# Layer 3 of a four-layer graph network: both of its weight products as seven block products, with the weight combinations streamed from DRAM

## Chip, core and metric

The kernel runs on one core of a Trainium2 chip. The metric is the device time of one execution in microseconds (us). Everything is 32-bit floating point.

TensorE (PE in the profile) multiplies, VectorE (DVE), ScalarE (ACT) and GpSimd (POOL) do the elementwise work, and SyncE (SP) issues DMA transfers. Products land in PSUM, eight banks of 128 partitions x 512 floats; everything else lives in SBUF.

## What is computed

The input x has 128 graphs of 64 nodes with 512 features. Four graph layers run one after the other, each followed by a residual and a layer norm:

```
x = layernorm(x + L0(x, adj, w, a))            # attention from one score per node
x = layernorm(x + L1(x, adj, Wq, Wk, Wv, ...)) # attention from x Wq Wk^T x^T, times adj
x = layernorm(x + L2(x, adj, mask, Wqk, Wv))   # softmax over nodes, scales x Wv
x = layernorm(x + L3(x, adj, W1, b1, gamma, beta, W2, b2))
```

Layer 3 is what the change is about. With H = (adj != 0) and the degree factors D and B:

```
def hypergraph_conv(x, adj, W, b):
    xw = x @ W.T
    m = Be * (H.T @ xw)
    return Dn * (H @ m) + b
h = relu(hypergraph_conv(x, adj, W1, b1))      # 512 -> 1024
h = layer_norm(h, gamma, beta)
y = hypergraph_conv(h, adj, W2, b2)            # 1024 -> 512
return y + x
```

## The kernel before

**Tiles and groups.** Two graphs make a tile of 128 nodes, two tiles (GT = 2) make a group of 256 nodes, and there are 32 groups (NG). `run(g)` at L361 is a generator that takes one group through all four layers. It stops at 15 yields, so it has 16 stages. Up to four groups are in flight (IN_FLIGHT), four stages apart (APART), and the main loop at L515 advances each of them by one stage in every step, the youngest first. So in one step in four the stages that stand side by side are, for example, the gather of layer 0, the scores of layers 1 and 2, and the first product of layer 3 (L485). Two steps later comes the second product of layer 3 (L506), beside the transposes of layers 1 and 2 (L278) and layer 2's product with its value weights (L464). One round of four steps finishes one group.

**Order of the instructions.** The program states only the operations and their buffers. A scheduler puts each engine's instructions in an order ahead of time, mostly by the order of the program but also by when it expects operands and buffers to be ready, and adds the waits. On the chip that order is fixed.

**Buffers.** A pool of n buffers under one name hands out a new buffer when an older one has been released by its last reader. In PSUM before the change: four buffers `mm` (the products), two `tr` (transposes and gathers), two `sm` (small results: scores, row sums, softmax), which are all eight banks.

**Layer 3 before.** `gathered(xt, gm)` at L470 multiplies the group's features by the normalised two-step adjacency `gm` and leaves the transposed result `gT`. The stage at L485 multiplies it by w3a, which lies in SBUF as a whole (512 x 1024): for each of two tiles and two halves of 512 columns, four matmuls over 128 rows of the weight. VectorE adds the bias, ScalarE applies the relu, VectorE takes the statistics. After the normalisation (L493) the gather at L502 makes `ghT`, and L506 multiplies by w3b (1024 x 512, in SBUF, with gamma folded in at L217): for each of two tiles eight matmuls of 512 columns. The result is added to `xt`, which already holds the residual (L472 to L477, on GpSimd). Then come the last layer norm and the store.

**Block-diagonal matrices.** The adjacency of a tile is two 64 x 64 blocks. Before the change three things are written as 128 x 128 block-diagonal tiles from standing sets of zeroed buffers: the attention weights of layers 0 and 1 (`e_bd`, three buffers, `on_diagonal` at L354), H for the product that makes `gm` (`h_bd`, two, L425), and `gm` itself (`g_bd`, three). `row_sums` at L324 sums over them with a matmul against ones.

**Every four groups** `prepare_chunk` at L232 prepares the adjacency of eight tiles. It needs four `mm` buffers through `over_graph` (L222).

Where a statement stands in a helper, the profile gives the helper's line: L296 is `product` (all products by w0, w_v1, w_v2, w3a, w3b), L305 `product_T` (the projections), L320 `scores`, L327 `row_sums`, L278 `transposed`, L288 `gathered`, L346 the end of `layer_norm`. L374 is layer 0's score product, L419 layer 1's product with the values, L440 the product of layer 2's softmax, L443 and L447 its maximum and exponential, L458 the product for `gm`.

Of the kernel before, what the change touches and what calls it, by code (L numbers as in the profile page):

```python
# [24 lines left out]
IN_FLIGHT = 4  # L25
EPS = 1e-5
# [5 lines left out]
def kernel(  # L32
# [31 lines left out]
    ps_mm = ctx.enter_context(tc.tile_pool(name="ps_mm", bufs=4, space=bass.MemoryType.PSUM))  # L64
    ps_tr = ctx.enter_context(tc.tile_pool(name="ps_tr", bufs=2, space=bass.MemoryType.PSUM))
    ps_sm = ctx.enter_context(tc.tile_pool(name="ps_sm", bufs=2, space=bass.MemoryType.PSUM))
# [33 lines left out]
    next_e = diagonals("e_bd", 3)  # L100
    next_h = diagonals("h_bd", 2)
# [46 lines left out]
    w3a_sb = weights(w3a, D, DH, "w3a_sb")  # L148
# [3 lines left out]
    w3b_sb = weights(w3b, DH, D, "w3b_sb")  # L152
# [56 lines left out]
    def prepare_3():  # L209

        ps = ps_mm.tile([P, D], FP, name="mm")
        for c in range(KH):
            nc.tensor.matmul(ps, beta_c[:, c : c + 1].to_broadcast([P, P]), w3b_sb[:, c, :],
                             start=(c == 0), stop=(c == KH - 1))
        nc.scalar.copy(bw_b, ps)
        for c in range(KH):
            nc.vector.tensor_scalar(w3b_sb[:, c, :], w3b_sb[:, c, :], gamma_c[:, c : c + 1], None, ALU.mult)  # L217
# [106 lines left out]
    def row_sums(bd):  # L324
        ps = ps_sm.tile([P, GT, P], FP, name="sm")
        for t in range(GT):
            nc.tensor.matmul(ps[:, t, 0:1], bd[:, t, :], ones, start=True, stop=True)  # L327
        return ps[:, :, 0]

# [31 lines left out]
    def run(g):  # L361
# [23 lines left out]
        nc.vector.reciprocal(f, row_sums(bd))  # L385
# [27 lines left out]
        bd = on_diagonal(next_e(), e, adj)  # L413
        yield
        f = small.tile([P, GT], FP, name="f")
        nc.vector.reciprocal(f, row_sums(bd))
        for t in range(GT):
            po = ps_mm.tile([P, D], FP, name="mm")
            nc.tensor.matmul(po, bd[:, t, :], v[:, t, :], start=True, stop=True)  # L419
            nc.vector.scalar_tensor_tensor(xt[:, t, :], po, f[:, t : t + 1], xt[:, t, :], ALU.mult, ALU.add)  # L420
        layer_norm(xt)

        h_bd = next_h()
        for rows, cols in halves:
            nc.vector.tensor_scalar(h_bd[rows, :, cols], adj[rows], 0.0, None, ALU.not_equal)  # L425
# [31 lines left out]
        for t in range(GT):  # L457
            nc.tensor.matmul(pg[:, t, :N], h_bd[:, t, :], bhd[:, t, :], start=True, stop=True)  # L458
# [13 lines left out]
        for t in range(GT):  # L472
            c = work.tile([P, D], FP, name="junk")
            nc.gpsimd.tensor_scalar(c, bw_b, g1[:, t : t + 1], 1.0, ALU.mult, ALU.mult)
            nc.gpsimd.tensor_add(c, c, b3b_b)
            nc.gpsimd.tensor_scalar(xt[:, t, :], xt[:, t, :], 2.0, 0.0, ALU.mult, ALU.add)  # L476
            nc.gpsimd.tensor_add(xt[:, t, :], xt[:, t, :], c)  # L477
        yield
        h = stage.tile([P, GT, DH], FP, name="h")
        st = small.tile([P, GT, DH // D, 6], FP, name="st3")  # L480
        mv = small.tile([P, GT, 2], FP, name="mv")
        for t in range(GT):
            for i in range(DH // D):
                hi = h[:, t, ts(i, D)]
                nc.vector.tensor_add(hi, product(gT, t, w3a_sb, ts(i, D)), b3a_b[:, ts(i, D)])  # L485
                nc.scalar.activation(hi, hi, AF.Relu)  # L486
                nc.vector.bn_stats(st[:, t, i, :], hi)  # L487
            nc.vector.bn_aggr(mv[:, t, :], st[:, t].rearrange("p i s -> p (i s)"))
# [8 lines left out]
        for t in range(GT):  # L497
            ghT.append(work.tile([P, KH, P], FP, name="ghT"))
            for i in range(KH // KC):
# [3 lines left out]
                nc.scalar.copy(ghT[t][:, ts(i, KC), :], tr)  # L503
        yield
        for t in range(GT):
            nc.vector.tensor_add(xt[:, t, :], product(ghT[t], 0, w3b_sb, chunks=KH), xt[:, t, :])  # L506
# [8 lines left out]
    while g < NG or running:  # L515
# [14 lines left out]
        if step == 4:  # L530
            prepare_2()
        if step == 7:
            prepare_3()
# [42 lines left out]
```

## Time and profile before

| | us |
|---|---|
| median of three runs | 2632.75 (2632.62 to 2634.61) |
| profiled execution | 2635.76 |
| its span in the profile | 2634.0 |
| DVE L342, the layer norms' statistics, x256 | 176.0 |
| DVE L346, their last step, x256 | 185.3 |
| DVE L485, bias of the first product, x128 | 88.5 |
| DVE L487, its statistics, x128 | 88.8 |
| DVE L506, end of the second product, x64 | 44.3 |
| POOL L402, L474, L475, L476, L477 together | 351.8 |
| ACT L503, copies of ghT, x128 | 75.0 |
| mean clock of TensorE | 0.998 of full |

A row of a group gives line, engine, operation, what it writes and reads (names without buffer numbers), the shapes and the count; then its busy time, the mean duration in ns, and after the second bar how long the engine had stood idle just before these instructions and what ended most of that. PE is TensorE's matmuls, PEld its weight loads, which overlap them. A row of the timeline starts with the start and the length of a run of equal instructions. A row of the chain has the same two numbers and what was on the path. A row of the view of windows has the stretch, its length, and for PE, PEld, DVE, ACT and POOL in turn the busy time with the count of instructions, then TensorE's clock, the share of DMA and its GB/s.

DMA is nearly unused after the start: 19 GB/s on average, 217 in the first fortieth of the span.

### The profile page before, as it was taken

How to read it: one execution, taken by the hardware profiler on the slowest of the kernel's cores; microseconds unless marked ns; L12 is line 12 of the kernel's file. 1: busy time of each engine (PE TensorE's matmuls, PEld its weight loads, DVE VectorE, ACT ScalarE, POOL GpSimd, SP SyncE). 2: the span in 40 equal slices, each digit the busy share in tenths (PEclk: the TensorE clock that was granted, in tenths of full speed). 3: DMA queues.
4: the chain of work that ended last, by engine and by line, in shares of the span. 5: the costliest groups of instructions: out<-in, count | busy, mean ns of one | idle time of the engine just before them, and what ended most of it. 6: DMA issues, size and time to landing. Idle time of an engine off the chain costs nothing.

```text
span 2634.0 us, 27593 instructions
## 1 busy us (share of the span) xinstructions
PE 2556.3 (97%) x11272; PEld 1544.1 (59%) x11272; DVE 1138.0 (43%) x2552; ACT 590.6 (22%) x1164; POOL 546.8 (21%) x560
## 2 busy tenths in 40 slices
PE   6999999999999999999999999999999999999998
PEld 4565565655565655565655565655665655665654
DVE  3535453445433455433545434445443445433443
ACT  0222221222221222221122221222221222221221
POOL 4211221212211222211312212212212212211211
PEclk9999999999999999999999999999999999999999
DMA  5000000000000000000000000000000000000000
GB/s 217 32 1 17 5 17 17 16 17 13 8 16 17 21 17 8 10 17 20 17 16 4 14 21 17 17 17 1 17 16 17 17 17 0 17 16 8 9 9 16
DMA packets 22190, 50.31 MB, mean 19 GB/s; under 512 B 1504, under 2 KB 1504, under 8 KB 22064
## 3 DMA queue, kind: packets, MB, share of 16 engines
q1 hardware_dynamic: 18560, 35.66, 4.0%
q0 software_dynamic: 3504, 12.89, 1.3%
q8 instruction: 89, 1.46, 0.2%
q14 instruction: 37, 0.30, 0.0%
HBM read 31.76 MB, written 16.78 MB: 18 GB/s over the span
## 4 chain that ended last, share of the span: by engine, by line
PE 87%; DVE 5%; issue 5%; POOL 3%; DMA 0%; ACT 0%; POOLq 0%; DVEq 0%
PE mm L296 57%; PE mm L305 17%; PE tr L288 4%; PE sm L320 2%; POOL rstd L335 2%; DVE x L346 2%; PE tr L278 1%; DVE x L420 1%; PE mm L169 1%; PE mm L225 1%; DVE x L389 1%; PE mm L419 1%; PE sm L327 1%; PE sm L374 0%; DMA junk<-in_a_dram 0%
## 5 line engine op out<-in xcount | busy, mean ns | idle before, releaser
L296 PE MATMUL mm<-wv_sb,xT 128*128 128x512 f32 x1024 | 460.6, 593 | 0.0
L305 PE MATMUL mm<-xT,m_sb 128*128 128x256 f32 x2048 | 458.3, 381 | 2.1 <-DVE hw L254 1.5
L296 PE MATMUL mm<-w3a_sb,xT 128*128 128x512 f32 x1024 | 448.0, 595 | 0.0
L296 PE MATMUL mm<-w3b_sb,ghT 128*128 128x512 f32 x1024 | 444.7, 592 | 0.0
L305 PEld LDWEIGHTS mm<-xT,m_sb 128*128 128x128 f32 x2048 | 385.7, 190 | 70.8 <-issue 17.9
L335 POOL TENSOR_TENSOR rstd<-ve,mhalf 128x2 f32<-128x2 f32 x160 | 127.7, 798 | 1369.9 <-DVE ve L333 1291.0
L296 PEld LDWEIGHTS mm<-w3b_sb,ghT 128*128 128x128 f32 x1024 | 194.5, 190 | 244.4 <-issue 244.4
L296 PEld LDWEIGHTS mm<-w3a_sb,xT 128*128 128x128 f32 x1024 | 191.9, 190 | 231.7 <-issue 229.6
L296 PEld LDWEIGHTS mm<-wv_sb,xT 128*128 128x128 f32 x1024 | 187.2, 190 | 185.8 <-issue 183.9
L385 DVE RECIPROCAL f<-sm 128x2 f32<-128x2 f32 x32 | 5.5, 171 | 617.9 <-PE sm L327 617.9
L296 PE MATMUL mm<-w_sb,xT 128*128 128x512 f32 x512 | 225.2, 593 | 0.4 <-issue 0.4
L346 DVE TENSOR_SCALAR x<-x,mv,rstd 128x512 f32<-128x512 f32 x256 | 185.3, 765 | 75.2 <-POOL rstd L335 75.2
L342 DVE BATCH_NORM_STATS2 st<-x 128x6 f32<-128x512 f32 x256 | 176.0, 688 | 4.7
L485 DVE TENSOR_TENSOR h<-mm,b3a_b 128x512 f32<-128x512 f32 x128 | 88.5, 692 | 193.4 <-PE mm L296 193.4
L296 PEld LDWEIGHTS mm<-w_sb,xT 128*128 128x128 f32 x512 | 97.0, 190 | 122.3 <-issue 122.2
L486 ACT ACTIVATE h<-h 128x512 f32<-128x512 f32 x128 | 80.6, 630 | 387.7 <-DVE h L485 387.7
L506 DVE TENSOR_TENSOR x<-mm,x 128x512 f32<-128x512 f32 x64 | 44.3, 691 | 277.0 <-PE mm L296 277.0
L476 POOL TENSOR_SCALAR x<-x 128x512 f32<-128x512 f32 x64 | 39.7, 620 | 559.9 <-PE tr L288 559.9
L502 PE MATMUL tr<-g_bd,h 128*128 128x128 f32 x1024 | 125.7, 282 | 5.5 <-ACT h L493 5.5
L487 DVE BATCH_NORM_STATS2 st<-h 128x6 f32<-128x512 f32 x128 | 88.8, 694 | 88.4 <-ACT h L486 88.4
L309 ACT ACTIVATE z<-mm,r_c 128x256 f32<-128x256 f32 x128 | 60.6, 473 | 293.7 <-PE mm L305 293.7
L502 PEld LDWEIGHTS tr<-g_bd,h 128*128 128x128 f32 x1024 | 121.3, 195 | 7.7 <-ACT h L493 7.4
(138 smaller groups left out, 2374.4 us busy)
## 6 DMA issues: line engine op xcount, KB each, us to landing
x<-in_x_dram SPq DMA_DIRECT2D x32, 512.0 KB, 3.7
out_dram<-x SPq DMA_DIRECT2D x32, 512.0 KB, 2.8
adj<-in_adjT_dram SPq DMA_DIRECT2D x8, 256.0 KB, 2.8
wv_sb<-in_wv_dram POOLq DMA_DIRECT2D x2, 1024.0 KB, 15.3
w3a_sb<-in_w3a_dram POOLq DMA_DIRECT2D x1, 2048.0 KB, 17.4
w3b_sb<-in_w3b_dram POOLq DMA_DIRECT2D x1, 2048.0 KB, 16.4
h<-in_wqk_dram POOLq DMA_DIRECT2D x2, 1024.0 KB, 5.7
w_sb<-in_w_dram POOLq DMA_DIRECT2D x1, 1024.0 KB, 10.7
```

Source lines behind the costliest of these rows:

```text
L288: nc.tensor.matmul(tr[:, c, :], xt[:, t, ts(c, P)], bd[:, t, :], start=True, stop=True)
L296: nc.tensor.matmul(ps, lhsT[:, k, ts(t, P)], w[:, k, cols], start=(k == 0), stop=(k == chunks - 1))
L305: nc.tensor.matmul(pz[:, : GT * P], w[:, k, ts(c, P)], xT[:, k, :], start=(k == 0), stop=(k == KC - 1))
L309: nc.scalar.activation(zT[:, c, :], pz[:, : GT * P], AF.Identity, bias=bias[:, c : c + 1])
L320: nc.tensor.matmul(ps[rows, t, :N], zT[:, k, tok], xT[:, k, tok], start=(k == 0), stop=(k == KC - 1))
L335: nc.gpsimd.tensor_tensor(rstd, ve, mhalf, ALU.pow)
L342: nc.vector.bn_stats(st[:, t, :], xt[:, t, :])
L346: nc.vector.tensor_scalar(xt[:, t, :], xt[:, t, :], mv[:, t, 0:1], rstd[:, t : t + 1], ALU.subtract, ALU.mult)
L485: nc.vector.tensor_add(hi, product(gT, t, w3a_sb, ts(i, D)), b3a_b[:, ts(i, D)])
L486: nc.scalar.activation(hi, hi, AF.Relu)
L487: nc.vector.bn_stats(st[:, t, i, :], hi)
L502: nc.tensor.matmul(tr[:, c, :], h[:, t, ts(i * KC + c, P)], gm[:, t, :], start=True, stop=True)
```

## The change

Each product of layer 3 is divided into 2 x 2 blocks: the two tiles of the group by two halves of the input features on the left, two halves of the input features by two halves of the output columns on the right. Four output blocks would need eight block products. The change uses Winograd's form of Strassen's scheme, with seven products of sums of blocks: four sums on the left (`side_sums`) and four on the right (`combined`).

- The sums of the weights are made once (`prepare_3a`, `prepare_3b`), written to DRAM, and from then on all weight blocks are streamed: `fetch` issues on SP's queue the next of 14 pieces a group, 512 KB each, into a ring of six. The piece that follows six later is requested when a product has been issued. The two whole weights leave SBUF.
- `side_sums` makes the sums of the left side, three on VectorE and one on GpSimd, into parts of the tile `h` that are free at that time. It stands at the end of the stage before the product.
- `seven_products` keeps two PSUM accumulators (`chx`, `chz`, one bank each) over several products and reads the partial sums in between, and takes one `mm` buffer for a third. VectorE adds seven results to the four output blocks.
- PSUM: `mm` has three buffers, `chx` and `chz` one each, `tr` two, `sm` one.
- To make room, `h_bd` and one of the `e_bd` buffers go. Layer 1's attention and H stay compact tiles of 64 columns, and row sums, layer 1's product with the values and the product for `gm` are done for the two halves of 64 partitions separately.

```diff
+RING = 6
+PIECE = 1024
-    ps_mm = ctx.enter_context(tc.tile_pool(name="ps_mm", bufs=4, space=bass.MemoryType.PSUM))
+    ring = ctx.enter_context(tc.tile_pool(name="ring", bufs=RING))
+    dram = ctx.enter_context(tc.tile_pool(name="dram", bufs=1, space=bass.MemoryType.DRAM))
+    ps_mm = ctx.enter_context(tc.tile_pool(name="ps_mm", bufs=3, space=bass.MemoryType.PSUM))
+    ps_ch = ctx.enter_context(tc.tile_pool(name="ps_ch", bufs=1, space=bass.MemoryType.PSUM))
-    ps_sm = ctx.enter_context(tc.tile_pool(name="ps_sm", bufs=2, space=bass.MemoryType.PSUM))
+    ps_sm = ctx.enter_context(tc.tile_pool(name="ps_sm", bufs=1, space=bass.MemoryType.PSUM))
-    next_e = diagonals("e_bd", 3)
-    next_h = diagonals("h_bd", 2)
+    next_e = diagonals("e_bd", 2)
-    w3a_sb = weights(w3a, D, DH, "w3a_sb")
-    w3b_sb = weights(w3b, DH, D, "w3b_sb")
...
+    USE = ("b11", "b21", "t2", "t1", "t3", "b22", "t4")
+    def combined(q):
+        t1, t2 = piece_tile(), piece_tile()
+        nc.gpsimd.tensor_sub(t1, q["b12"], q["b11"])
+        nc.vector.tensor_sub(t2, q["b22"], t1)
+        t3 = piece_tile()
+        nc.gpsimd.tensor_sub(t3, q["b22"], q["b12"])
+        t4 = piece_tile()
+        nc.vector.tensor_sub(t4, q["b21"], t2)
+        return {"t1": t1, "t2": t2, "t3": t3, "t4": t4}
...
+    def fetch():
+        n = fetched[0]
+        fetched[0] += 1
+        if n >= NG * 2 * len(USE):
+            return
+        which = "ab"[n // len(USE) % 2]
+        src = pieces[which][USE[n % len(USE)]]
+        t_ = piece_tile()
...
+        nc.sync.dma_start(out=dst, in_=src)
+        on_chip.append(t_)
...
-    def row_sums(bd):
+    def row_sums(e):
         ps = ps_sm.tile([P, GT, P], FP, name="sm")
         for t in range(GT):
-            nc.tensor.matmul(ps[:, t, 0:1], bd[:, t, :], ones, start=True, stop=True)
+            for h, (rows, _) in enumerate(halves):
+                nc.tensor.matmul(ps[rows, t, 0:1], e(t, h), ones[rows], start=True, stop=True)
         return ps[:, :, 0]
+
+    def side_sums(s, a):
+        nc.vector.tensor_add(s[0], a["21"], a["22"])
+        nc.gpsimd.tensor_sub(s[2], a["11"], a["21"])
+        nc.vector.tensor_sub(s[1], s[0], a["11"])
+        nc.vector.tensor_sub(s[3], a["12"], s[1])
+
+    def seven_products(a, s, base, dst):
+        n = a["11"].shape[1]
+        def times(ps, left, first, last):
+            b = on_chip.popleft().rearrange("p (c o) -> p c o", c=n)
+            for k in range(n):
+                nc.tensor.matmul(ps, left[:, k, :], b[:, k, :], start=first and k == 0, stop=k == n - 1,
+                                 skip_group_check=True)
+            fetch()
+        w = PIECE // n
+        x = ps_ch.tile([P, D], FP, name="chx")[:, :w]
+        y = ps_mm.tile([P, D], FP, name="mm")[:, :w]
+        z = ps_ch.tile([P, D], FP, name="chz")[:, :w]
+        add = nc.vector.tensor_add
+        times(x, a["11"], True, False)
+        add(dst["11"], x, base["11"])
+        times(y, a["12"], True, True)
+        add(dst["11"], y, dst["11"])
+        times(x, s[1], False, False)
+        add(dst["12"], x, base["12"])
+        times(z, s[0], True, False)
+        add(dst["22"], z, base["22"])
+        times(x, s[2], False, False)
+        add(dst["22"], x, dst["22"])
+        times(z, s[3], False, True)
+        add(dst["12"], z, dst["12"])
+        times(x, a["22"], False, True)
+        add(dst["21"], x, base["21"])
...
-        bd = on_diagonal(next_e(), e, adj)
+        nc.vector.tensor_mul(e, e, adj)
         yield
         f = small.tile([P, GT], FP, name="f")
-        nc.vector.reciprocal(f, row_sums(bd))
+        nc.vector.reciprocal(f, row_sums(lambda t, h: e[halves[h][0], t, :]))
         for t in range(GT):
             po = ps_mm.tile([P, D], FP, name="mm")
-            nc.tensor.matmul(po, bd[:, t, :], v[:, t, :], start=True, stop=True)
+            for rows, _ in halves:
+                nc.tensor.matmul(po[rows], e[rows, t, :], v[rows, t, :], start=True, stop=True)
...
-            nc.tensor.matmul(pg[:, t, :N], h_bd[:, t, :], bhd[:, t, :], start=True, stop=True)
+            for rows, _ in halves:
+                nc.tensor.matmul(pg[rows, t, :N], hT[rows, t, :], bhd[rows, t, :], start=True, stop=True)
...
-        yield
+
         h = stage.tile([P, GT, DH], FP, name="h")
+        a = {f"{t + 1}{i + 1}": gT[:, ts(i, KC // 2), ts(t, P)] for t in range(GT) for i in range(2)}
+        room = [h[:, 1, ts(i, D // 2)].rearrange("p (k q) -> p k q", q=P) for i in (2, 3, 0, 1)]
+        side_sums(room, a)
+        yield
+        blocks = {f"{t + 1}{i + 1}": h[:, t, ts(i, D)] for t in range(GT) for i in range(2)}
+        seven_products(a, room, {k: b3a_b[:, ts(int(k[1]) - 1, D)] for k in blocks}, blocks)
...
-                nc.vector.tensor_add(hi, product(gT, t, w3a_sb, ts(i, D)), b3a_b[:, ts(i, D)])
...
-        yield
-        for t in range(GT):
-            nc.vector.tensor_add(xt[:, t, :], product(ghT[t], 0, w3b_sb, chunks=KH), xt[:, t, :])
+        a = {f"{t + 1}{i + 1}": ghT[t][:, ts(i, KC), :] for t in range(GT) for i in range(2)}
+        room = [h[:, t, ts(i, D)].rearrange("p (k q) -> p k q", q=P) for t in range(GT) for i in range(2)]
+        side_sums(room, a)
+        yield
+        blocks = {f"{t + 1}{i + 1}": xt[:, t, ts(i, D // 2)] for t in range(GT) for i in range(2)}
+        seven_products(a, room, blocks, blocks)
         layer_norm(xt)
```

## The prediction

> **What bounds the kernel now.** I read the page's first part, then its groups, then the chain of waits over one steady round, then the timeline of the tightest stretch. The page and the groups of TensorE:
>
> ```profile
> PE 2556.3 (97%) x11272; PEld 1544.1 (59%) x11272; DVE 1138.0 (43%) x2552; ACT 590.6 (22%) x1164; POOL 546.8 (21%) x560
> ...
> L296 PE MATMUL mm<-w3a_sb,xT 128*128 128x512 f32 x1024 | 448.0, 595 | 0.0
> L296 PE MATMUL mm<-w3b_sb,ghT 128*128 128x512 f32 x1024 | 444.7, 592 | 0.0
> ...
> L278 PE MATMUL tr<-ident,x 128*128 128x128 f32 x512 | 77.9, 276 | 41.6 <-DVE x L346 41.6
> ```
>
> TensorE is busy 97% of the span and the two products of layer 3 are 893 us of it. Its only steady stop is before the second transposes, L278: 41.6 us, or 1.3 us for each of the 32 groups. One f32 matmul is two instructions, hence 1024 for 512 calls. So time is gained only by taking matmul time away, and lost by any new stop of TensorE. Pieces of the chain between 1299 and 1394 us (start, length, what), which hold one round of 79.05 us (first w3a matmul at 1313.13 and 1392.18 us):
>
> ```profile
> 1300.94 6.91 PE mm L305 x32
> ...
> 1311.19 2.02 PE sm L320 x64
> ...
> 1334.00 0.34 PE sm L327 x4
> 1334.34 1.82 PE mm L419 x4
> 1336.16 0.22 PE sm L440 x2
> 1336.38 0.41 PE sm L458 x4
> ...
> 1365.02 0.38 PE sm L374 x8
> 1365.40 7.10 PE mm L305 x32
> 1372.51 6.87 PE mm L296 x16
> 1379.37 6.91 PE mm L305 x32
> ```
>
> From them come the prices: an instruction with 512 columns 6.87/16 = 0.429 us, with 256 columns 6.91/32 = 0.216 us (half, so narrower products lose nothing), a score instruction on 64 columns of the array 2.02/64 = 0.032 us. Last, the timeline after the attention of layer 1 and a count of the busy time around it:
>
> ```profile
> 1336.00 0.38 PE L440 MATMUL sm<-e,same 128*128 128x128 f32 x2
> 1336.22 0.56 PE L458 MATMUL sm<-bhd,h_bd 128*128 128x64 f32 x4
> ...
> 1340.21 0.27 DVE L443 TENSOR_REDUCE mx<-sm 128x2 f32<-128x128 f32 x1
> ...
> 1341.45 0.54 ACT L447 ACTIVATE e<-sm,mx 128x64 f32<-128x64 f32 x2
> ...
> 1342.48 2.88 DVE L346 TENSOR_SCALAR x<-x,mv,rstd 128x512 f32<-128x512 f32 x2 [0.58 <-POOL rstd L335]
> ...
> 1344.10 0.63 PE L278 MATMUL tr<-ident,x 128*128 128x128 f32 x4 [1.91 <-DVE x L346]
> ```
>
> ```profile
> 1334.00:1349.50 15.50, 13.59 (x76) 9.26 (x75) 13.86 (x34) 5.53 (x12) 8.86 (x9) 1.00 0.00 1
> ```
>
> The reader is to see that L458 runs 5.8 us before the softmax has finished with the tile that L440 wrote; that TensorE then stands until the layer norm is out; and that VectorE (third count of the second fence) is full there, 13.86 of 15.5 us, though only 43% over the span.
>
> **What the Trainium skill says.** "TensorEngine Tiling (Array Packing)", Key Properties: the quarters of the array work independently, and a change of tiling mode drains the engine. The trace agrees for half-width tiles: 64 score instructions of 64 columns take 2.02 us, where 0.429/8 = 0.054 us each would be 3.4 us, so two run side by side. It also shows the drain: L374's 8 instructions take 0.38 instead of 0.25 us and the L305 block behind them 7.10 instead of 6.91, so one visit to another mode costs 0.32 us. Quarters of 64x64 are not in this trace. "TensorE: Matmul & The Clock Gate", Step-by-step: matmuls stay in program order, only weight loads are pulled ahead; so one waiting matmul holds all behind it. "SBUF — State Buffer", Who interferes with whom: VectorE operations with two SBUF inputs contend with GpSimd's reads. The trace agrees: L346 takes 2.88 us for two beside L402 on POOL, and 1.00 us without it.
>
> **The change part by part, per group.**
>
> *Products.* w3a: 32 instructions become 7x2x2 = 28, 4 x 0.429 = 1.72 us saved. w3b: 32 x 0.429 = 13.73 becomes 7x4x2 = 56 x 0.216 = 12.10, 1.63 saved. Together 3.35, x32 = 107 us. This is the whole gain.
>
> *Array quarters.* Row sums (twice), the attention product L419 and the product for gm, L458, become pairs of 64x64. If pairs run side by side as the score halves do, L419 keeps its 4 x 0.429; row sums go from 0.34 to 8 x 0.032 = 0.25, gm from 0.41 to 0.25. That saves 0.34. Two new visits to another mode in this stretch (row sums with L419; gm) cost 2 x 0.32; the first row sum stands next to the scores, which pay the visit already. Net +0.3, x32 = +10. Bounds: -0.34 if no drain is seen (-11), and +2.4 if quarters run one after another (second rival).
>
> *One sm buffer instead of two.* In the stretch at 1311 us row sums, first scores and second scores now each wait for a reader: L385 (0.17 us) and L412 (0.54 us for two), each with about 0.3 us to start and 0.2 back. The program order isn't kept strictly (two of the w_v2 instructions stand between the transposes, and gather instructions between projections), so the first w3a products can fill these waits; then scores are visited separately, two visits more, 0.64 us. Either way I take 0.7, +22. Bounds 0 and 1.5 (+48). The same rule moves gm's product behind L447: first rival.
>
> *Waits in the chain of seven.* A partial sum must be read before the next product is added to it, and the other accumulator's product lies between: 4 x 0.429 = 1.72 us. The reader starts 0.31 us after the slot's end and takes 0.69 (L485, 692 ns), and TensorE starts 0.18 after a release (L346 half-way at 1343.92, L278 at 1344.10). Slack 0.54 us; for 256 columns 0.42 us in place of 0.69, slack 0.8. VectorE works about 40% of that time on these reads, the normalisation statistics beside them (0.69 each) cannot be interrupted. Four such waits a product; I take 0.3 for both, +10; bounds 0 and, if each of eight overran by 0.3, 2.4 (+77).
>
> *VectorE and POOL.* Added: 7 instead of 4 reads of 0.69 (+2.1), 7 of about 0.42 instead of 2 of 0.69 (+1.6), three sums of 256 (about 0.4 each) and three of 512 (about 0.69 each), +3.3; gone: one L357 and one L425 half, about 1. Net +6 us of 79, which takes VectorE to near 52%: no bound over a round. In the full stretch, however, the side sums of the second product (2.1 us, more where POOL holds the port: L402, L474 and L475 run there, plus the new subtraction, 1.27 by L475) fall where the layer norm and softmax are awaited. The earlier end of h_bd gives about 1.2 back. I take 0.7 more of stop at L278 or at the third product of w3b, +22; bounds 0 and 2 (+64). The side sums of the first product lie in 1372 to 1386 us and after, where VectorE is idle.
>
> *Weights by DMA.* 14 pieces of 512 KB a group; the same size lands in 3.7 us for x, so even one at a time 52 us of 76. Six are in the ring; the seventh of a product is requested after the first is used (1.72 us), lands by about 6, and is wanted at 6 x 1.72 = 10.3: 4 us to spare. Between the products lie over 20 us. On SP's queue the output store waits for the last layer norm (1369.02) and the x load for that store, but both come after the fetches of their round and 20 us before the next. Cost nothing; if the cover failed, each late piece would stop TensorE outright.
>
> *mm with three buffers.* The products and projections read theirs within 1.7 us, so three suffice. The four matmuls of a chunk (L225) take all four now; with three the last waits for a 3.3 us reciprocal (L250). About 1 us for each of 8 chunks, +8.
>
> *Start and end.* The combinations are made while TensorE has other work; the last group has nothing to hide its reads, +5.
>
> Sum: -107+10+22+10+22+8+5 = -30. On the profiled execution's 2635.76 us (span 2634.0 and 1.8 around it) this is 2606; the median, 2632.75, lies 3 lower: 2603.
>
> **The rivals.**
>
> First, slower: gm's product stands on TensorE's queue directly behind L440, as now, and has to wait for its buffer. L440 ends at 1336.4 and the exponentials at 1342.0: 5.7 us of stop. The present stop of 1.3 at L278 is used up in it, so 4.4 net, 141 over 32 groups. A schedule that stops there needs no extra visits to another mode and no extra stop at L278 (22+22 of my sum), so -30-44+141 = +67: 2700. If half of the wait is filled by the 3.6 us of L502, 2665. It decides from about 0.9 us of net stop a group over my sum (30/32). For it: L458 is second behind L440 today, and VectorE reaches L443 late. Against: waiting matmuls are passed by others in several places today.
>
> Second, slower: quarters run one after another. L419 8 x 0.429 instead of 4 (+1.72), row sums and gm +0.7: 2.4 x 32 = 77, 2680. Half-width tiles speak against it.
>
> Third, nothing gained: port contention and the chain's reads both near their upper bounds (+54 and more) leave the gain below 0.2%.
>
> Fourth, better: extra stops are all filled; -107+10+8+5 = -84, 2549.
>
> **How the numbers follow.** Likeliest, a gain of 15 to 80 us (2553 to 2618): 0.47. Better than that: 0.05. A gain of 5 to 15: 0.03. Within 0.2% (5 us, about what a measurement tells from none): 0.05. First rival 0.24, second 0.08, other stops that exceed the gain 0.08. Faster 0.55, same 0.05, slower 0.40. The range 2553 to 2690 leaves out the better case and the far end of the slower ones.
>
> **What would show it.** w3a instructions 896 and w3b 1792 with 256 columns, together about 107 us less busy. L419's successors: 256 instructions at the same busy time if quarters pair. The idle before gm's product and before L278 tells the first rival. No idle of TensorE on DMA. VectorE near 1330 us busy. Wrong if a wait inside the seven products exceeds 1 us a group.

## The result, and the profile after

| | before | after |
|---|---|---|
| median, us | 2633.67 | 2670.56 (2667.16 to 2674.82) |
| after / before | | 1.0141, 95% interval 1.0123 to 1.0159 |
| profiled execution, us (span) | 2635.76 (2634.0) | 2671.21 (2669.4) |

The kernel became 1.4% slower; 2603 us, a gain of 1.1%, was forecast. The matmul time was saved as forecast. More than that was lost in and just before one place, the second transposes, and in TensorE's clock just behind it.

First, from the page of after: the busy times of the engines, TensorE's granted clock in forty slices, and the row of the second transposes (busy us and mean ns of one, then idle time before it and what ended it).

```profile
PE 2530.7 (95%) x12440; PEld 1669.1 (63%) x12440; DVE 1376.6 (52%) x2948; ACT 593.3 (22%) x1164; POOL 624.1 (23%) x623
...
PEclk9999999999999999999999999999999999999998
...
L352 PE MATMUL tr<-ident,x 128*128 128x128 f32 x512 | 101.1, 322 | 74.8 <-DVE x L460 74.8
```

The row before had L278 at 77.9 us busy with 41.6 us of idle ahead of it. Now L352, the same 512 transposes, is 101.1 us busy, 322 ns each instead of 276, and its idle time is 74.8 us. Two things changed at once: the stop became longer, and the work behind it slower. The products by w_v1 and w_v2, whose matmuls the change doesn't touch, became slower too (before, then after):

```profile
L296 PE MATMUL mm<-wv_sb,xT 128*128 128x512 f32 x1024 | 460.6, 593 | 0.0
```

```profile
L370 PE MATMUL mm<-wv_sb,xT 128*128 128x512 f32 x1024 | 495.1, 628 | 0.0
```

The clock row shows next to nothing, since a slice is 67 us long: a tenth is the finest that it tells.

Second, groups of TensorE with different shapes kept apart, columns as above: part of the seven products, the attention product, the product for gm and one product of a chunk.

```profile
L420 PE MATMUL chx<-piece,h 128*128 128x512 f32 x256 | 122.6, 598 | 2.6 <-DVE h L430 2.6
...
L420 PE MATMUL chz<-piece,h 128*128 128x256 f32 x512 | 121.0, 379 | 0.0
...
L534 PE MATMUL mm<-z,e 64*64 64x512 f32 x256 | 61.2, 597 | 0.0
L420 PE MATMUL mm<-piece,ghT 128*128 128x256 f32 x256 | 60.5, 379 | 0.0
...
L573 PE MATMUL sm<-bhd,hT 64*64 64x64 f32 x256 | 14.3, 231 | 14.0 <-ACT e L561 14.0
...
L299 PE MATMUL mm<-md,same 128*128 128x512 f32 x16 | 9.9, 704 | 7.3 <-DVE hw L328 7.3
```

These rows answer to the first three steps of the prediction. The instructions of the second product (L420 with 256 columns, four such groups in all, 1792 instructions) take 379 ns each, as the 256-column projections do, so nothing is lost by the narrower shape. 256 instructions of 64 x 64 do L534's work in 61.2 us, where 128 of the whole array took 62.8 before:

```profile
L419 PE MATMUL mm<-z,e_bd 128*128 128x512 f32 x128 | 62.8, 613 | 0.0
```

So quarters of the array run side by side. Inside the seven products TensorE waited 2.6 us in all, for the read L430, and nowhere on DMA. A new wait is L573's, 14.0 us for the exponentials of L561. The chunks' products wait 7.3 us for a reciprocal, in two waits, of which one in the first chunk is 5.3 us.

Third, the timeline of after around one stop (start, length, engine, line, what; in brackets idle time before it). These are lines on GpSimd, VectorE, ScalarE and TensorE from the moment in which the last gathered block is copied:

```profile
1443.10 1.44 POOL L409 TENSOR_TENSOR h<-ghT 128x512 f32<-128x512 f32 x1 [2.26 <-ACT ghT L623]
...
1443.32 1.24 DVE L447 TENSOR_SCALAR ve<-mv 128x2 f32<-128x2 f32 x1
...
1444.49 1.26 POOL L516 TENSOR_TENSOR x<-x,bv_b 128x512 f32<-128x512 f32 x1
1444.54 1.76 DVE L466 SCALAR_TENSOR_TENSOR junk<-x,u_b 128x512 f32<-128x512 f32 x1
1444.66 0.52 ACT L561 ACTIVATE e<-sm,mx 128x64 f32<-128x64 f32 x2 [0.33 <-DVE mx L558]
...
1445.23 0.45 PE L573 MATMUL sm<-bhd,hT 64*64 64x64 f32 x8 [0.49 <-ACT e L561]
...
1445.61 0.44 PE L352 MATMUL tr<-ident,x 128*128 128x128 f32 x2
1445.71 1.15 POOL L449 TENSOR_TENSOR rstd<-ve,mhalf 128x2 f32<-128x2 f32 x1
...
1446.90 2.31 DVE L460 TENSOR_SCALAR x<-x,mv,rstd 128x512 f32<-128x512 f32 x2 [0.58 <-POOL rstd L449]
...
1448.52 1.08 PE L352 MATMUL tr<-ident,x 128*128 128x128 f32 x4 [2.47 <-DVE x L460]
```

The reader follows the chain from top to bottom. GpSimd's new subtraction L409 runs from 1443.10 to 1444.54. VectorE's small L447, 0.17 us with no GpSimd operation beside it, begins at 1443.32 inside it and ends with it, 1.24 us later. GpSimd then takes the bias addition L516, which was ahead in its queue, and only at 1445.71 the rstd that L447 had made possible. The normalisation L460 can begin at 1446.90 and meets the second L516, so that it takes 2.31 us for two. TensorE, which has had nothing since 1446.05 but waits for L460, goes on at 1448.52. "SBUF — State Buffer", section Who interferes with whom, says that a VectorE tensor_scalar that runs in a two-port mode and a GpSimd instruction block each other fully. The trace doesn't name the mode, but L447 (0.17 us alone, 1.24 us beside L409) and L460 (1.00 us for two alone, 2.31 here) behave so.

Fourth, three stretches of the same place (length, busy time and count of PE, PEld, DVE, ACT, POOL; then PEclk, DMA share, GB/s). By the clock records of the trace the clock fell at 1447.57 and came back at 1454.40, so these limits lie 0.15 us late:

```profile
1444.31:1447.72 3.41, 1.25 (x13) 0.65 (x11) 2.83 (x5) 1.65 (x6) 3.41 (x4) 0.98 0.01 2
1447.72:1454.54 6.82, 6.02 (x14) 3.40 (x15) 5.36 (x15) 1.17 (x2) 3.11 (x4) 0.51 0.00 0
1454.54:1461.37 6.83, 6.83 (x25) 4.32 (x24) 4.10 (x10) 0.00 (x0) 2.25 (x3) 1.00 0.04 6
```

In the stretch with the stop the clock is still at full speed, but for those 0.15 us (PEclk 0.98). In the next, 6.82 us long, it is at half (0.51 with the same overlap), and once the stop is over, TensorE gets only 14 instructions done in the 6 us that remain. Then it is back. The clock changes in the trace on a fixed grid of 3.41 us. Over the whole run of after it is at half for 141.9 us in 31 falls. Of these, 26 follow one of the 31 longer stops at the second transposes; the other five lie at the start and the end. In before it is at half for 14.0 us, in two falls at the end.

### The profile page after: what moved, and what is told of

It reads as the page before. It is cut to its first block, busy times and chain, and to the rows that moved or that the text cites. A ratio compares the mean times of both kernels' runs of the same rounds, so it can differ in the third digit from the quotient of the medians.

```text
span 2669.4 us, 31726 instructions
## 1 busy us (share of the span) xinstructions
PE 2530.7 (95%) x12440; PEld 1669.1 (63%) x12440; DVE 1376.6 (52%) x2948; ACT 593.3 (22%) x1164; POOL 624.1 (23%) x623
## 4 chain that ended last, share of the span: by engine, by line
PE 83%; DVE 5%; POOL 3%; issue 3%; ACT 1%; POOLq 0%; DVEq 0%; ACTq 0%
PE mm L370 24%; PE mm L379 16%; PE chx L420 16%; PE chz L420 8%; PE mm L420 4%; PE tr L362 4%; PE tr L622 3%; PE sm L394 3%; DVE x L460 2%; PE tr L352 2%; PE mm L534 2%; POOL rstd L449 2%; POOL x L516 1%; DVE dn L324 1%; PE sm L403 1%
## 5 line engine op out<-in xcount | busy, mean ns | idle before, releaser
L370 PE MATMUL mm<-wv_sb,xT 128*128 128x512 f32 x1024 | 495.1, 628 | 0.0
L379 PEld LDWEIGHTS mm<-xT,m_sb 128*128 128x128 f32 x2048 | 387.5, 190 | 77.9 <-issue 19.0
L370 PEld LDWEIGHTS mm<-wv_sb,xT 128*128 128x128 f32 x1024 | 199.0, 203 | 193.9 <-issue 191.7
L408 DVE TENSOR_TENSOR h<-xT 128x256 f32<-128x256 f32 x32 | 29.9, 934 | 476.5 <-ACT xT L363 476.5
L420 PE MATMUL chx<-piece,h 128*128 128x256 f32 (+1 forms) x768 | 243.6, 452 | 2.6 <-DVE h L430 2.6
L420 PE MATMUL chz<-piece,h 128*128 128x256 f32 (+1 forms) x768 | 242.4, 452 | 0.0
L370 PE MATMUL mm<-w_sb,xT 128*128 128x512 f32 x512 | 226.8, 595 | 0.0
L460 DVE TENSOR_SCALAR x<-x,mv,rstd 128x512 f32<-128x512 f32 x256 | 175.9, 728 | 60.4 <-POOL rstd L449 60.4
L420 PEld LDWEIGHTS chz<-piece,h 128*128 128x128 f32 x768 | 146.6, 191 | 75.4 <-issue 62.2
L420 PEld LDWEIGHTS chx<-piece,h 128*128 128x128 f32 x768 | 145.4, 190 | 75.1 <-issue 52.3
L370 PEld LDWEIGHTS mm<-w_sb,xT 128*128 128x128 f32 x512 | 97.3, 191 | 121.4 <-issue 121.2
L352 PE MATMUL tr<-ident,x 128*128 128x128 f32 x512 | 101.1, 322 | 74.8 <-DVE x L460 74.8
L352 PEld LDWEIGHTS tr<-ident,x 128*128 128x128 f32 x512 | 71.7, 166 | 131.2 <-issue 109.0
L363 ACT COPY xT<-tr 128x512 f32<-128x512 f32 x128 | 72.1, 587 | 288.1 <-PE tr L362 176.3
L420 PE MATMUL chx<-piece,xT 128*128 128x512 f32 x256 | 129.7, 614 | 0.0
```

The costliest lines, as they stand in the source:

```text
L352: nc.tensor.transpose(tr[:, c, :], xt[:, t, ts(c, P)], ident)
L370: nc.tensor.matmul(ps, lhsT[:, k, ts(t, P)], w[:, k, cols], start=(k == 0), stop=(k == chunks - 1))
L379: nc.tensor.matmul(pz[:, : GT * P], w[:, k, ts(c, P)], xT[:, k, :], start=(k == 0), stop=(k == KC - 1))
L420: nc.tensor.matmul(ps, left[:, k, :], b[:, k, :], start=first and k == 0, stop=k == n - 1, skip_group_check=True)
L460: nc.vector.tensor_scalar(xt[:, t, :], xt[:, t, :], mv[:, t, 0:1], rstd[:, t : t + 1], ALU.subtract, ALU.mult)
```

## Where the 37 us went

The time from each TensorE instruction's start to the start of the next can be summed by line from the two traces. Unlike busy times, which overlap, these add up to the time from the first start to the last:

| us | before | after | difference |
|---|---|---|---|
| product by w3a (1024 / 896 instructions) | 447.8 | 414.6 | -33.2 |
| product by w3b (1024 / 1792) | 441.1 | 388.6 | -52.5 |
| products by w0, w_v1, w_v2 (1536, unchanged) | 665.9 | 698.8 | +32.9 |
| second transposes L278 / L352 (512, unchanged) | 100.0 | 168.5 | +68.5 |
| chunk products L225 / L299 | 31.5 | 41.2 | +9.7 |
| all others | | | +12 |
| sum | 2609.5 | 2646.9 | +37.4 |

The 68.5 at the transposes are the stop itself (from 42.4 to 75.2, +32.8), the new wait of gm's product, which in this order follows a transpose (29 times 0.65, +18.8, a visit to another array mode included), and 16.8 of half clock: 157 of the 512 transposes began at half clock and took 33.6 us from start to start, 0.21 each, where the others take 0.11. The products by w_v2 stand directly behind the stop and didn't change at all: the 33 us of their row are the half clock. So the stops cost 52 us more, and the clock about 50 (33 and 17).

## The experiments

Theories. *Clock*: the stop trips the clock, and its price is more than its length. *Stop only*: the stop costs its length; the clock is of no account. Then: which part of the change lengthens the stop (buffers, sums, quarters, streaming)? The mean of a stop is taken here over the 30 groups in which the second transposes have a full one. All ratios are against the kernel before on the same chips, whose median lay between 2633.99 and 2634.82 us.

**fill.** Spare matmuls behind gm's product fill the stop; the result isn't touched, but TensorE has more to do.

```diff
+        for _ in range(8):
+            nc.tensor.matmul(pg[:, 1, N:], same, eye, start=True, stop=True, skip_group_check=True)
```

> The changed kernel with eight spare matmuls of 64 columns (16 instructions, about 1.8 us) put on TensorE's queue behind the product for gm; TensorE's order is otherwise the same. Clock theory: in the changed kernel TensorE ran at half clock for about 142 us (14 before), and half of the surplus, 64 us, is lost; the spare work lies in the stop at the second transposes and keeps the engine busy, so the half-clock time falls to some 15 to 30 us and the time to about 2610 (2600 to 2620), though more is computed. Stop theory (the stop itself and the added work are the loss, the clock is incidental): the spare work only fills the stop, 2670, within 5 us.

Measured 2601.59 us (2599.40 to 2604.48), 0.9873 of before (0.9858 to 0.9888): 69 us less than after, with 512 instructions more. TensorE's groups in this run:

```profile
L370 PE MATMUL mm<-wv_sb,xT 128*128 128x512 f32 x1024 | 460.8, 592 | 0.0
...
L352 PE MATMUL tr<-ident,x 128*128 128x128 f32 x512 | 77.7, 274 | 5.4 <-DVE x L460 5.2
...
L575 PE MATMUL sm<-eye,same 128*128 128x64 f32 x512 | 63.9, 278 | 0.0
...
L573 PE MATMUL sm<-bhd,hT 64*64 64x64 f32 x256 | 14.3, 230 | 14.0 <-ACT e L561 14.0
```

The stop is filled (5.4 us of idle left) and gm's wait is as in after; the spare work takes 63.9 us where 72 us of stop are gone. Had only the stop's length counted, some 8 us would have been gained (13, with the spare work counted from start to start), not 69. L352 is at 274 ns again, L370 at 592, and the half clock has gone from 141.9 to 36.5 us. This is the run that decides for the clock theory: work that does nothing makes the kernel faster.

**sub_on_vector.** The second product's subtraction on VectorE; the order of TensorE's instructions is that of after.

```diff
-        nc.gpsimd.tensor_sub(s[2], a["11"], a["21"])
+        (engine or nc.gpsimd).tensor_sub(s[2], a["11"], a["21"])
...
-        side_sums(room, a)
+        side_sums(room, a, nc.vector)
```

> The changed kernel with the one subtraction on GpSimd for the second product moved to VectorE; TensorE's order is the same. Theory: the subtraction (1.44 us) stands ahead of the bias addition and of the reciprocal root on GpSimd and blocks VectorE's small operation for it, which makes the stop at the second transposes 2.5 us long and trips the clock; without it the stop is about 1 us, the half-clock time falls below 30 us, and the time to 2585 to 2610. Rival (VectorE is full in this stretch, so 0.7 us more of work on it lengthens the stop): 2670 to 2700.

Measured 2568.91 us (2567.69 to 2572.71), 0.9747 (0.9730 to 0.9763), better than expected. TensorE's groups:

```profile
L370 PE MATMUL mm<-wv_sb,xT 128*128 128x512 f32 x1024 | 462.2, 595 | 0.0
...
L352 PE MATMUL tr<-ident,x 128*128 128x128 f32 x512 | 84.2, 279 | 33.9 <-DVE x L460 33.9
```

One instruction a group put on another engine is worth 102 us. The stop falls from 2.51 to 1.14 us in the mean, gm's wait is nearly gone (1.9 us of idle time left), the clock is at half for 32.8 us, and the products by w0 and w_v are back at 666.5 us from start to start. Summed from start to start, the gain is 41 us of stop, 12 of gm's wait, and 17 and 32 of half clock. VectorE, the fuller of the two engines, was the better place: what counted was the subtraction's time on the port and in GpSimd's queue ahead of the rstd. Which of these two does more was not separated.

**before_pools.** The kernel before with three mm buffers and one sm buffer, nothing else.

```diff
-    ps_mm = ctx.enter_context(tc.tile_pool(name="ps_mm", bufs=4, space=bass.MemoryType.PSUM))
+    ps_mm = ctx.enter_context(tc.tile_pool(name="ps_mm", bufs=3, space=bass.MemoryType.PSUM))
...
-    ps_sm = ctx.enter_context(tc.tile_pool(name="ps_sm", bufs=2, space=bass.MemoryType.PSUM))
+    ps_sm = ctx.enter_context(tc.tile_pool(name="ps_sm", bufs=1, space=bass.MemoryType.PSUM))
```

> The kernel before with three mm buffers instead of four and one sm instead of two, nothing else. TensorE's order then has the product for gm in the middle of the first transposes, as in the changed kernel, and scores between the first product's matmuls. Theory (buffers cost the wait for the exponentials, 0.65 us a group, the separate visits, about 0.6, and the chunk's fourth product): +40 us, 2665 to 2685, half clock still below 30 us. Rival (the buffers alone make the stop that trips the clock): half clock above 100 us and 2720 or more. Rival (waits are all filled): within 8 us of before.

Measured 2743.93 us (2743.22 to 2748.36), 1.0422 (1.0406 to 1.0437). My expectation was missed by 59 us and the rival's held. The two rows that hold the new idle time:

```profile
L305 PE MATMUL mm<-xT,m_sb 128*128 128x256 f32 x2048 | 467.5, 387 | 19.5 <-DVE dn L251 19.5
...
L278 PE MATMUL tr<-ident,x 128*128 128x128 f32 x512 | 93.4, 303 | 63.3 <-DVE x L346 63.3
```

The stop rises to 2.13 us in the mean, and the clock falls 33 times (126.8 us at half), 22 of them behind a stop at the second transposes: the buffers alone are enough to trip it. A second wait appears at the projections (L305, 19.5 us, six times behind a chunk). The order of TensorE's instructions isn't that of before here, so what comes of the mm buffer, of the sm buffer and of the new order stays open.

**before_sums.** The kernel before with the second product's four side sums added and not used.

```diff
...
+        nc.vector.tensor_add(s[0], a["21"], a["22"])
+        nc.gpsimd.tensor_sub(s[2], a["11"], a["21"])
+        nc.vector.tensor_sub(s[1], s[0], a["11"])
+        nc.vector.tensor_sub(s[3], a["12"], s[1])
```

> The kernel before with the four side sums of the second product added (three on VectorE, one on GpSimd, results not used); TensorE's order is that of before. Theory: the GpSimd subtraction lengthens the stop at the second transposes from 1.4 to about 2.5 us and the half-clock time rises from 14 to 80 us or more: +35 for stops and +30 to 60 for the clock, 2700 to 2730. Rival (the stop needs the single sm buffer as well): stop grows by 1.1 us, clock stays, 2670. Rival (the sums are hidden): 2640.

Measured 2691.24 us (2689.83 to 2692.93), 1.0218 (1.0203 to 1.0234), somewhat below the expectation. The second transposes here:

```profile
L278 PE MATMUL tr<-ident,x 128*128 128x128 f32 x512 | 86.1, 297 | 72.8 <-DVE x L346 72.8
```

The sums make the stop as long as in after (2.45 us in the mean), and the clock is at half for 71.7 us, with 19 falls. None of the four added instructions is TensorE's, and its order is that of before, yet they cost 57 us: from start to start 31 of stop, 8 in the other transposes and 20 in the products by w_v, and next to nothing elsewhere.

**before_quarters.** The kernel before with 64 x 64 row sums, attention product, gm product and H only.

```diff
-            nc.tensor.matmul(po, bd[:, t, :], v[:, t, :], start=True, stop=True)
+            for rows, _ in halves:
+                nc.tensor.matmul(po[rows], e[rows, t, :], v[rows, t, :], start=True, stop=True)
```

> The kernel before with row sums, layer 1's product with the values and the product for gm on halves of 64 partitions and compact tiles, nothing else. If pairs of quarters run side by side: L534's like takes the same 62 us as before, two visits more cost 0.6 a group, row sums and gm save 0.3, so +10, 2640 to 2650. If one after another: +77, 2710. H in one VectorE operation instead of two may shorten the stop at the second transposes a little.

Measured 2631.14 us (2630.13 to 2635.84), 0.9993 (0.9986 to 0.9999): within what can be told from no change, below the expectation. The stop went from 1.41 to 1.14 us in the mean, which is some 8 us and hides about 5 of cost in the rest of TensorE's work; why the stop is shorter was not followed up. The quarters are no cause of the loss.

**no_stream.** After without any fetch beyond the first six pieces: the later weight combinations are left out and those six used again.

> The changed kernel in which after the first six pieces nothing is fetched: the ring's six tiles are reused without a transfer, so the weights of both products are left out (wrong ones stand in). If the transfers cost nothing: 2665 to 2675. If late pieces or port traffic cost time: 2650 or less.

Measured 2669.50 us (2666.85 to 2674.70), 1.0138 (1.0123 to 1.0153), with the stop at 75.2 us as in after. Streaming 14 pieces a group costs nothing.

**sm_two.** After with two mm and two sm buffers.

```diff
-    ps_mm = ctx.enter_context(tc.tile_pool(name="ps_mm", bufs=3, space=bass.MemoryType.PSUM))
+    ps_mm = ctx.enter_context(tc.tile_pool(name="ps_mm", bufs=2, space=bass.MemoryType.PSUM))
...
-    ps_sm = ctx.enter_context(tc.tile_pool(name="ps_sm", bufs=1, space=bass.MemoryType.PSUM))
+    ps_sm = ctx.enter_context(tc.tile_pool(name="ps_sm", bufs=2, space=bass.MemoryType.PSUM))
```

> After with two mm and two sm buffers, as the kernel before has them; nothing else changed. Clock theory, if the buffers are what lengthens the stop: gm's product no longer waits for the exponentials (0.65 us a group), the scores need fewer visits of their own (some 0.6 us a group), the stop at the second transposes falls below 2 us in most groups, half clock 30 to 90 us instead of 142, time 2600 to 2645. Rival (the added sums lengthen the stop, the buffers don't matter): the stop stays near 2.5 us, half clock 120 to 150, time 2655 to 2675.

Measured 2632.47 us (2630.95 to 2637.63), 0.9997 (0.9988 to 1.0006): 38 us below after, and level with before. The time was expected, its reason only in part:

```profile
L370 PE MATMUL mm<-wv_sb,xT 128*128 128x512 f32 x1024 | 485.8, 619 | 0.0
...
L352 PE MATMUL tr<-ident,x 128*128 128x128 f32 x512 | 88.5, 303 | 68.5 <-DVE x L460 68.5
...
L573 PE MATMUL sm<-bhd,hT 64*64 64x64 f32 x256 | 14.3, 230 | 0.0
```

gm's product no longer waits, but the stop stays at 2.30 us in the mean, where less than 2 was expected, and the clock still falls 26 times (101.7 us at half; L370 619 ns). So one mm buffer given for a second sm buffer gains about 38 us, and the sums keep the clock falling without the single sm. Added alone to before, each of the two parts trips the clock (before_pools, before_sums). Undone alone in after they differ: the second sm buffer leaves the falls, while moving the one subtraction (sub_on_vector) ends them but for two in the first 190 us, with the single sm buffer still there.

**before_transposes_late and transposes_late.** Layer 2's second transposes one stage later, in before and in after.

```diff
-        xT = transposed(xt)
         yield
+        xT = transposed(xt)
```

> The kernel before with the same move of layer 2's transposes. Its stop there was 42 us in all and its half-clock time only 14 us, so about 2592 (2585 to 2605). If the stop moves elsewhere, 2630.

> The changed kernel with layer 2's transposes issued one stage later, before its projection, so that 14 us of other TensorE work lies between the layer norm and them. Clock and stop theory: the stop of 2.5 us and the half clock both go; 2670 less 64 for the clock less 75 for the stops is about 2530 (2520 to 2560). Rival (the loss is in extra visits to another array mode and in waits inside the seven products): no stop is left to remove beyond the 75 us, 2595 and no less.

Before: 2602.01 us (2599.89 to 2603.75), 0.9874 (0.9859 to 0.9888), as expected: the stop of before was worth 32 us and could be had without the change. After: 2624.56 us (2621.41 to 2624.97), 0.9957 (0.9942 to 0.9972), where 2520 to 2560 was expected. The stop has moved. Two groups of TensorE with shapes kept apart, then VectorE's timeline of one round:

```profile
L420 PE MATMUL chx<-piece,h 128*128 128x256 f32 x512 | 127.9, 394 | 58.5 <-DVE x L430 58.5
...
L352 PE MATMUL tr<-ident,x 128*128 128x128 f32 x512 | 77.8, 277 | 0.0
```

```profile
1424.46 1.23 DVE L447 TENSOR_SCALAR ve<-mv 128x2 f32<-128x2 f32 x1
...
1425.68 1.76 DVE L466 SCALAR_TENSOR_TENSOR junk<-x,u_b 128x512 f32<-128x512 f32 x1
...
1428.03 2.32 DVE L460 TENSOR_SCALAR x<-x,mv,rstd 128x512 f32<-128x512 f32 x2 [0.59 <-POOL rstd L449]
...
1438.00 0.42 DVE L430 TENSOR_TENSOR x<-chx,x 128x256 f32<-128x256 f32 x1
```

No idle time is left before L352, but the second product's third part waits 58.5 us for the read L430 of its first. VectorE works from 1418.27 to 1438 without a gap longer than 0.6 us, with the same L447 of 1.23, a row dot of 1.76 and L460 of 2.32 us in it, and comes to L430 at 1438.00. So the transposes look like no more than the first to wait for VectorE's backlog.

**dots_later.** That is tested by sub_on_vector with layer 1's row dots and bias additions in the next stage, and there behind the product's last read (VectorE) and the last rstd (GpSimd).

```diff
-        d = small.tile([P, GT], FP, name="d")
-        for t in range(GT):
-            row_dot(d[:, t : t + 1], xt[:, t, :], 1.0, u1_b)
...
         yield
+        d = small.tile([P, GT], FP, name="d")
+        with behind("vector"):
+            for t in range(GT):
+                row_dot(d[:, t : t + 1], xt[:, t, :], 1.0, u1_b)
+            nc.vector.tensor_scalar(d, d, c1_c, None, ALU.add)
+        with behind("pool"):
+            for t in range(GT):
+                nc.gpsimd.tensor_add(xt[:, t, :], xt[:, t, :], bv1_b)
```

> After with the second product's subtraction on VectorE, and layer 1's row dots and bias additions moved one stage later, behind the last read of the product (VectorE) and the last rstd (GpSimd); TensorE's instructions in the same order as after. Clock theory with VectorE's backlog as the cause of the stop: stop at the second transposes under 0.7 us a group, half clock under 30 us, time 2540 to 2560. Rival (the rest of the stop is the chain read, statistics, rstd, normalisation itself): stop near 1.1 us as in sub_on_vector, 2565 to 2575.

Measured 2523.70 us (2523.05 to 2524.44), 0.9579 (0.9563 to 0.9594), below the expected range. TensorE's order is that of after but for the start and the chunks (228 of 12440 places). Groups, and the timeline at the place shown of after:

```profile
L370 PE MATMUL mm<-wv_sb,xT 128*128 128x512 f32 x1024 | 460.8, 593 | 1.8 <-ACT z L383 1.8
...
L352 PE MATMUL tr<-ident,x 128*128 128x128 f32 x512 | 77.9, 276 | 2.4 <-DVE x L465 2.4
```

```profile
1363.85 0.69 DVE L409 TENSOR_TENSOR h<-ghT 128x512 f32<-128x512 f32 x1 [0.17 <-ACT ghT L629]
...
1364.46 0.17 DVE L452 TENSOR_SCALAR ve<-mv 128x2 f32<-128x2 f32 x1
...
1364.71 0.69 POOL L454 TENSOR_TENSOR rstd<-ve,mhalf 128x2 f32<-128x2 f32 x1 [3.01 <-DVE mx L564]
...
1365.43 1.00 DVE L465 TENSOR_SCALAR x<-x,mv,rstd 128x512 f32<-128x512 f32 x2
...
1366.05 0.87 PE L352 MATMUL tr<-ident,x 128*128 128x128 f32 x6
```

The idle time before L352 is 2.4 us in the whole run. In the timeline L452 (L447 of after) takes 0.17 us, the rstd follows at once (0.69), and L465 (L460 of after) takes 1.00 us for two with no bias addition beside it. The last transposes start at 1366.05, before the normalisation's second half is even out. Half clock is 32.8 us, all of it in the first 85 and the last 45 us. Which of the two moves does more, dots or bias additions, was not separated.

**dots_later_transposes_late and before_dots_later_transposes_late.** Both moves together, in after and in before.

> The run dots_later, and layer 2's second transposes moved behind the stage boundary. With VectorE's backlog gone, the third product's read is no longer late, so the wait that took the stop's place in transposes_late (68 us in all) falls under 15 us; half clock 20 to 35 us; time 2525 to 2550. Rival (the third product waits for its own read whatever VectorE has queued): 2560 or more.

> The kernel before with the same two moves (row dots and bias additions later, second transposes later). It had 42 us of stops there and 14 us at half clock; before_transposes_late gave 2602 with the late transposes alone. Both theories: 2590 to 2603. The gap to dots_later_transposes_late is then what the seven products give once neither kernel stops: by the prediction's terms without the stop 107-10-10-8 = 79 less some extra visits, 50 to 75 us expected.

After: 2516.46 us (2515.50 to 2517.15), 0.9551 (0.9536 to 0.9566), the fastest of all runs and below the expected range; of the wait of transposes_late 2.6 us are left. Before: 2595.45 us (2593.51 to 2596.41), 0.9850 (0.9834 to 0.9865), as expected. From the page of the first:

```profile
PE 2467.7 (98%) x12440; PEld 1643.0 (65%) x12440; DVE 1331.2 (53%) x2980; ACT 583.2 (23%) x1164; POOL 576.7 (23%) x591
...
PEclk8999999999999999999999999999999999999999
```

With neither kernel stopped at the second transposes, the change (with its subtraction on VectorE) is worth 2595.45 - 2516.46 = 79 us, 3.0%. The expectation gave 50 to 75 after an allowance for visits; the sum on record without its sm, VectorE and end terms gives the same 79, in part by chance, since the visits of the sm term are still there.

## Why the prediction was wrong, step by step

- *Products, -107.* Right for the work itself. w3b: 52.5 us saved where the step gives 52. w3a: 33 instead of 55; the missing 22 are waits and mode visits, of the kind that the sm step put there.
- *Array quarters, +10.* Right in mechanism: pairs run side by side, as "TensorEngine Tiling (Array Packing)", Key Properties, says of independent tiles. "All others" in the table is +12; alone on before the quarters, net of a stop that is 8 us shorter, cost nothing that can be measured. The rival in which quarters run one after another is refuted by L534.
- *One sm buffer, +22, and the first rival.* The visits came to about these 22. But gm's product also waits for L561, which the first rival had priced at 5.7 us a group. It waits 0.65, visit included, since the gather, six transposes and one matmul of w_v2 were put ahead of it: 18.8 us that the sum didn't hold. The wait needs both the single sm buffer and the subtraction on GpSimd, since it goes in sm_two and nearly goes in sub_on_vector. With the clock that the buffer helps to trip, and less what an mm buffer is worth, the second sm buffer is worth 38 (sm_two). The rival's 2665 for half of the wait doesn't follow from its own terms: half of 141 added to -30-44 is -4, about 2629.
- *Waits in the seven-chain, +10.* Too high: 2.6 us of idle time. Where VectorE is behind, as in transposes_late, this wait does come, 58.5 us.
- *VectorE and GpSimd, +22.* The place and the mechanism were named, the subtraction beside the layer norm included; the size was 33. VectorE was busy for 1376.6 us, not 1330. The prediction put L346 under the rule of "SBUF — State Buffer", Who interferes with whom, for two SBUF inputs; L346 reads one tensor, and that section's rule on two-port modes is the one that can fit it. The rule for two inputs fits the row dot L466: 0.68 us in the median with no GpSimd operation beside it, 1.76 beside L516 and the rstd.
- *DMA, 0.* Right (no_stream).
- *mm with three buffers, +8.* Right in size, +9.7 at the chunks, but in part by luck: 5.3 of it is one wait in the first chunk.
- *Start and end, +5.* Not seen as such: the wait before the last group's gather is 5.6 us, and was 5.1 in before.

The step that failed is the pricing of the stop at L278: "I take 0.7 more of stop at L278" costed it at its length, and the sum has no term for the clock, which is put at nothing without a reason. The two stops, at the second transposes and before gm's product, grew by 52 us instead of 22. That alone, 30 us more, would have taken the whole gain and still left no loss. The other 50 are the half clock. fill removes them without removing any work, and the product rows behind the stop, 698.8 us in after and 665.9 in before, show 33 of them without any model.

That 2670 lies inside the recorded range (2553 to 2690) is luck. The rivals that reach so high do it by other ways: a net stop of 4.4 us before gm's product, quarters one after another, or waits inside the seven products near their bounds. The runs show 0.65 us, pairs side by side and 2.6 us in all. The third rival's port contention was there, and it too was priced by length alone.

"TensorE: Matmul & The Clock Gate", Part 1, What's actually happening, describes a half-rate state that comes after an idle window of about 3.4 us of a free-running monitor. The trace agrees on the half rate and the 3.41-us grid. It disagrees on what suffices: the stop is 2.5 us long in the mean, and the window that trips it isn't idle. In the round shown, TensorE streamed columns for a quarter of the window from 1444.16 to 1447.57, the last before the fall. (This share is an estimate worked out from the trace: 0.427 us for an instruction of 512 columns and in proportion for others, half of the 0.853 us that lies between the starts of two at half clock; at full clock 0.429 is measured. Quarters side by side count once.)

The warning stood in the profile of before. In the very round that the prediction shows, the window from 1342.0 to 1345.4 has a share of 38%, and the clock stayed; the lowest of that run is 37.5%. The kernel was at the edge, and the stop was read as 1.3 us of cost when it was also the margin.

## What to carry to other kernels

Where TensorE is the bound and has a steady stop, look at how much it streams in the clock's window around the stop, before anything is put on an engine that the stop waits for: past a limit, a microsecond of stop cost nearly two here (52 us of stop, 50 of clock). A small operation on the way to the stop, here a single rstd, should not stand behind long ones on its engine's queue or share a port with them; moving the bias additions, and VectorE's row dots with them, by a stage brought 45 us more than the first repair. And when a stop is moved instead of its cause removed, the next reader of the same late engine takes it over.

## What the runs showed of the hardware

- The clock. In all 14 traces taken together, with 185 falls, the granted clock fell to half after windows of 3.41 us in which TensorE streamed at most 0.379 of the time (worked out as above), and stayed after windows with at least 0.375. It came back after windows with at least 0.782 (worked out at half clock) and stayed low up to 0.778. So the limit for the fall lies near 0.38 and that for the return near 0.78. In after, a fall lasted one window or two, 3.4 or 6.8 us.
- A VectorE operation on 128 x 2 numbers (L447 of after), 0.17 us in the median with no GpSimd operation beside it, took 1.23 us in the median of the 29 times that it began inside the GpSimd subtraction L409 of about 1.43 us, and ended with it.
- Four groups of small products put on 64 x 64 quarters, with the visits to that mode, changed the kernel before by no more than 0.14% (before_quarters), a second-transposes stop that is 8 us shorter included.
